# Six multiplications first, then the transfers of the next gates: reordering one stretch of a windowed-attention and expert layer

## The chip, the cores and the metric

The kernel runs on one core of one Trainium2 chip. The metric is the device time of one execution in microseconds. The kernel before was run three times: 4276.44, 4277.0 and 4289.2 us, median 4277.0. One more execution was taken with the profiler; all readings of a trace are of that one.

## The reference

The input is an image of 2 x 128 channels x 256 x 256 in f32. One layer is computed, everything in f32:

```python
x = x + attention(_ln_c(x))      # normalized over the 128 channels
t = _to_tokens(x)                # 131072 tokens of 128 channels
t = t + experts(_ln_t(t))
```

`attention` projects queries, keys and values by 1x1 convolutions. Queries stand in windows of 8 x 8 pixels, keys and values in windows of 12 x 12 around them, four heads of 32. Relative position terms are added, and a fixed mask lets a query see only the keys of its own row and column parity, so that each window falls into four independent ones of 16 queries and 36 keys. A softmax, the weighted values and an output projection follow. `experts` is a router over 8 experts: the softmax of `x @ router_w`, the two largest kept and scaled to sum 1, and

```python
out = sum over e of gate[e] * (x @ expert_w[e])
```

## The kernel before, in words

The image is cut into 64 strips of 8 rows; because of the mask a strip is worked in 4 *planes*, one for each parity of row and column, 512 pixels each. The loop at L980 runs over the 256 planes `n`. The bodies of one turn belong to different planes, so that the engines have something else to do while one of them waits: attention of plane `n` (`scores`, `attend`, `out_project`), the projections of plane `n+1` (`project`), the norms and the routing of a row pair of the strip before (`norms`, `route`), and the experts of row pairs that were routed one and two turns earlier (`ex`, `nxt`, `new`).

The order on every engine is the order of the code: the loop stands under a manual schedule for all five engines, and each engine takes its instructions in turn. All transfers of the loop are issued by SyncE (SP), also in turn. A transfer that waits for something holds back all behind it in SP's queue.

The experts are done without a gather. For a row pair (512 tokens), the gates are written to DRAM as rows of 512 values (`spread`, tile `gd`: 8 rows of gates, one for the mean, one for the rates of another row pair's norm). Each row is then read back to all 128 partitions, 256 KB a time:

- `fetch_rstd` (L629, tile `rb`): the rates, 1/deviation, with which GpSimd normalizes a row pair for the attention (`ln1`, L236).
- `fetch_means` (L658, tile `sb`, one buffer): the row that is added to the tokens to subtract their mean.
- `fetch(e)` (L652 and L653, tile `gb`, 8 buffers): gate `e`. Ahead of the transfer stands a tiny write to the tile, a memset on VectorE or a copy on ScalarE. It holds the transfer back until that engine has come to this place.

One turn later `means` (L663) makes `xs = tokens + sb`, `times(e)` (L669) makes `xe = xs * gb[e]` on VectorE for e = 0, 1, 2, 3, 4, 6 and on GpSimd for 5 and 7, and `product(e)` (L678) multiplies `xe` with the expert's matrix on TensorE, all eight accumulating in one PSUM tile. `end` (L684) adds the sum to the tokens.

The values of the attention also take a way through DRAM: `send_values` (L329) stores the value rows of plane `n+1` in `vrows`, and `take_values` (L341, two transfers of 240 KB, pieces of 512 bytes) gathers them by window in `vwin`, from which the next turn's `attend` reads them (L485).

TensorE's instruction stream is long: each plane has 128 small matmuls in `scores` (L454) and 128 in `attend` (L485). `nc.tensor.addr_align(BLOCK, ...)` at L995 pads the stream with NOPs so that the code of each turn stands at the same place within blocks of 256 instructions.

The turn's stretch that the change touches is this (L1039 to L1050): it follows `shift` (VectorE, L352 and L357) and the start of `attend` (the sums matmul L475 on TensorE), and is followed by the rest of `attend`, the load of new image rows (L117), gate 3, the store of finished rows (L716) and gates 4 and 6; gates 5 and 7 follow at the head of the next turn.

Of the kernel before, what the change touches and what calls it, by code (L numbers as in the profile page):

```python
# [52 lines left out]
def kernel(  # L53
# [270 lines left out]
    def send_values(n, sent):  # L324

        i, pl = divmod(n, 4)
        for part, vr in sent:
            for k, at, m in runs(i, part):
                nc.sync.dma_start(  # L329
                    vrows[pl][1 : PC + 1, at : at + m, :],  # L330
                    vr[:, k - part[0] : k - part[0] + m],
                )
# [92 lines left out]
    def scores(n, state):  # L425


        qs, kk, au = state["qs"], state["kk"], state["au"]
        turn = place(n // 4, 0) // 2
        att = ps_att.tile([P, 4, 512], F32, tag="att", name=f"att{n}")  # L430
        sc = att[:, :, 0:HQ]
        for w in range(2):
            for half in range(2):
                rows = slice(half * SLOT, (half + 1) * SLOT)
                for h in range(HEADS):
                    hp = slice(h * DH, (h + 1) * DH)
                    nc.tensor.matmul(  # L437
                        sc[rows, h].rearrange("p (t w z) -> p t w z", w=2, z=16)[:, :, w],
                        lhsT=keys[hp, turn, w],
                        rhs=au[hp, half * NP + w : (half + 1) * NP : 2].rearrange(  # L440
                            "p t a s -> p t (a s)"
                        ),
                        start=(w == 0),
                        stop=False,
                    )
        for t in range(HP):
            if t == HP // 2:
                yield
            for h in range(HEADS):
                hp = slice(h * DH, (h + 1) * DH)  # L450
                for half in range(2):
                    rows = slice(half * SLOT, half * SLOT + NK)
                    m0 = 2 * (half * HP + t)
                    nc.tensor.matmul(  # L454
                        sc[rows, h, 32 * t : 32 * t + 32],
                        lhsT=kk[hp, half * HP + t, 0:NK],
                        rhs=qs[hp, m0 : m0 + 2].rearrange("p m a s -> p (m a s)"),
                        start=False,
                        stop=(t == HP - 1),
                    )  # L460
        pT = work.tile([P, HEADS, HQ], F32, tag="pT", name=f"pT{n}", bufs=1)
        nc.scalar.activation(pT, att[:, :, 0:HQ], AF.Exp)  # L462
        state.update(att=att, pT=pT)
        yield
# [44 lines left out]
    def out_project(n, state):  # L509

        i, pl = divmod(n, 4)
        po = mm_tile(f"po{n}")
        nc.tensor.matmul(  # L513
            po, lhsT=wo, rhs=state["o"].rearrange("p f z -> p (f z)"), start=True, stop=True
        )
        yield
        xv = xt[i].rearrange("p (a y) (m s x) -> p y x m a s", y=2, x=2, s=4)[:, pl // 2, pl % 2]
        nc.vector.tensor_add(xv, po.rearrange("p (m a s) -> p m a s", a=PR, s=4), xv)
        yield
# [92 lines left out]
    def spread(f, c, g, nm):  # L612

        gT = small.tile([P, 2, 32], F32, tag="gT", name=f"gT{nm}")
        nc.vector.transpose(
            gT.rearrange("p k i -> p (k i)"), g.rearrange("p k b j -> p (k b j)")
        )
        gd = dram.tile([2 * E * NT, P], F32, tag="gd", name=f"gd{nm}")

        to = gd.rearrange("(k j t) (b i) -> k (t b) j i", k=2, j=E, i=32)  # L620
        for k in (1, 0):
            if k or f:
                nc.sync.dma_start(to[k], gT[:, k])
        return gd
# [262 lines left out]
    def row_at(n):  # L887

        i, pl = divmod(n + 2, 4)
        for j, k in ((i + 1, pl + 2), (i + 2, pl - 2)):
            if 0 < j < len(strips) and k in ln_rows(j) and (k > 1 or strips[j][1] == 0):
                return j, k
        return None
# [78 lines left out]
    gated, ex, nxt = None, NoExperts(), NoExperts()  # L974
    last = ctile([P, 1], "last")
    pool, dve = nc.gpsimd, nc.vector

    ET = mybir.EngineType
    with tc.manual_schedule(engines={ET.PE, ET.DVE, ET.Activation, ET.Pool, ET.SP}):
        for n in range(n_planes):  # L980
            i, pl = divmod(n, 4)
            score, attn, outp, ahead, norm, rout = none, none, none, none, none, none
            if n < n_planes:
                score = scores(n, states[n])
                attn = attend(n, states[n])
                outp = out_project(n, states[n])
            if n + 1 < n_planes:
                states[n + 1] = {}
                ahead = project(n + 1, states[n + 1])

            late = n == 6 or n > 6 and row_at(n) is None
            if n > 6 and row_at(n - 1) is not None:
                nc.tensor.addr_align(BLOCK, offset=BLOCK - FIRST_LIMIT)  # L995


            next(score, None)
            new, row = NoExperts(), None
            if gated and gated[0]:  # L1000
                rout = route(*gated[0], *gated[2])
            next(rout, None)
            nxt.fetch(5, nc.scalar)
            for _ in rout:
                pass
            next(score, None)
            next(ahead, None)
            nxt.fetch(7, nc.scalar)
            if gated:
                f, c, made = gated  # L1010
                gd = spread(f, c, made[0], f"_{n}")
                new = Experts(*f, gd) if f else new
            if n + 1 < n_planes:
                send_values(n + 1, states[n + 1]["sent"])
            if gated and c:
                row = (*c, fetch_rstd(gd, f"_{n}"))
            next(ahead, None)
            if n + 1 < n_planes:
                states[n + 1]["shift"]()
            filling = n < FILL  # L1020
            if not filling:
                next(ahead, None)
                next(ahead, None)
            for e in (4, 6, 7, 5):
                ex.product(e)
            if late:
                nc.tensor.addr_align(BLOCK, offset=SUMS_AT)


            f = (i - 1, pl) if 0 < i <= len(strips) else None  # L1030
            c = row_at(n)
            if f or c:
                room = None
                if filling:
                    room = ps_acc.tile([P, 512], F32, tag="acc", name=f"plt_{n}")
                norm = norms(f, c, f"_{n}", room)
            next(norm, None)
            next(attn, None)
            nxt.means()  # L1039
            new.fetch_means()  # L1040
            if n + 1 < n_planes:
                take_values(n + 1)
            for e in (0, 1, 2, 3):
                nxt.times(e, dve)
            new.fetch(0, dve)
            for e in (4, 6):
                nxt.times(e, dve)
            new.fetch(1, dve)
            ex.end()
            new.fetch(2, dve)  # L1050
            next(attn, None)
            next(attn, None)


            ex = nxt
            next(norm, None)
            if filling:
                next(ahead, None)
                next(ahead, None)
            load_x((n + 9) // 4, (n + 9) % 4, paced=True)  # L1060
            new.fetch(3, dve)
            while to_store:
                store(*to_store.pop())
            next(ahead, None)
            ex.product(0)
            made = next(norm, None)
            ex.product(1)
            ex.product(2)
            new.fetch(4, nc.scalar)
            nxt.behind(6)  # L1070
            nxt.times(5, pool)
            if row:
                ln1(*row, pool)
            if pl == 3 and i + 2 < len(strips):
                halo(i + 2)
            nxt.times(7, pool)
            if n + 2 < n_planes:
                borders(n + 2)
            next(outp, None)
            ex.product(3)  # L1080
            next(outp, None)
            new.fetch(6, dve)
            gated, nxt = (f, c, made) if made else None, new
            states.pop(n, None)

        finish_last(ex, nxt, gated)
# [59 lines left out]
```

## Time and profile before

| | |
|---|---|
| time, median of three runs | 4277.0 us |
| profiled execution: its time | 4283.76 us |
| profiled execution: its span | 4281.9 us |
| mean granted TensorE clock | 0.995 |
| TensorE busy | 4207.7 us, 98% |
| VectorE busy | 3787.3 us, 88% |
| ScalarE busy | 1315.1 us, 31% |
| GpSimd busy | 1072.3 us, 25% |
| moved by DMA | 1022.15 MB, 239 GB/s |
| a turn of the loop, median | 16.25 us |

The span runs from the first instruction to the last; the time of an execution holds about 2 us around it. A busy share of the whole span says which engine is used most, not where it waits: for that the waits, the chain of work that ended last and the timeline are read. In a line of waits stand the engine and the line that waited, what ended the wait, the total in us, how often, and the longest one. "issue" as the cause means that the engine waited for no semaphore that the profile shows.

### The profile page before, as it was taken

What the parts mean: (1) busy time and instruction counts of PE and PEld (TensorE: products, weight loads), DVE (VectorE), ACT (ScalarE), POOL (GpSimd) and SP (SyncE); (2) the same over time, 40 slices, a digit from 0 to 9 for tenths busy, and PEclk for the clock granted to TensorE, in tenths of its full rate; (3) what the DMA queues carried; (4) which work ended last, traced back from release to release, by engine and by line L of the source; (5) the groups of instructions that cost most, each with busy time, mean ns of one, the idle gap of its engine ahead of it and who ended that gap; (6) DMA issues with size and microseconds to landing.
All of it is one profiled execution on the core that took longest, in us unless ns stands there. A gap on an engine that the chain in (4) does not pass through costs nothing.

```text
span 4281.9 us, 224026 instructions
## 1 busy us (share of the span) xinstructions
PE 4207.7 (98%) x94273; PEld 2456.8 (57%) x94273; DVE 3787.3 (88%) x11768; ACT 1315.1 (31%) x3750; POOL 1072.3 (25%) x1109
## 2 busy tenths in 40 slices
PE   7999999999999999999999999999999999999998
PEld 5555555555555555555555555555555555555554
DVE  5888988989889898889888889898889998998998
ACT  3332323233333333333333333333333333233320
POOL 1222222222222222222222222222222222222220
PEclk9999999999999999999999999999999999999999
DMA  4877877878777877787878787877787777778776
GB/s 117 243 233 239 245 242 242 247 239 250 238 245 241 250 237 246 237 246 238 251 237 246 238 247 241 248 238 244 238 248 239 248 243 244 245 243 246 239 233 219
DMA packets 824576, 1022.15 MB, mean 239 GB/s; under 512 B 137634, under 2 KB 409634, under 8 KB 823594
## 3 DMA queue, kind: packets, MB, share of 16 engines
q1 hardware_dynamic: 822864, 1007.52, 76.1%
q8 instruction: 769, 12.60, 1.3%
q14 instruction: 213, 1.74, 0.1%
q10 hardware_dynamic: 730, 0.29, 0.0%
HBM read 863.78 MB, written 143.75 MB: 235 GB/s over the span
## 4 chain that ended last, share of the span: by engine, by line
PE 97%; issue 1%; DVE 1%; DMA 1%; SPq 0%; ACT 0%; DVEq 0%
PE acc L678 41%; PE att L454 8%; PE att L485 7%; PE pv L310 7%; PE plt L544 6%; PE pu L369 5%; PE po L513 5%; PE pk L383 5%; PE pq L408 5%; PE att L437 4%; PE att L475 3%; PE accl L766 0%; DMA gl<-gd_l 0%; DMA gb<-gd 0%; PE pltn L253 0%
## 5 line engine op out<-in xcount | busy, mean ns | idle before, releaser
L678 PE MATMUL acc<-xe,ew 128*128 128x512 f32 x4016 | 1874.6, 598 | 5.5 <-issue 5.0
L678 PEld LDWEIGHTS acc<-xe,ew 128*128 128x128 f32 x4016 | 740.6, 189 | 902.6 <-issue 852.2
L669 DVE TENSOR_TENSOR xe<-xs,gb 128x512 f32<-128x512 f32 x1508 | 932.5, 685 | 8.6
L673 POOL COPY last<-xe 128x1 f32<-128x1 f32 x250 | 45.9, 184 | 3021.0 <-DVE gb L652 3021.0
L669 POOL TENSOR_TENSOR xe<-xs,gb 128x512 f32<-128x512 f32 x500 | 635.8, 1272 | 1.5 <-PE att L485 1.2
L454 PE MATMUL att<-qs,kcol 32*60 32x32 f32 x32768 | 394.4, 222 | 24.2 <-issue 23.8
L454 PEld LDWEIGHTS att<-qs,kcol 32*60 32x60 f32 x32768 | 388.5, 126 | 28.9 <-issue 27.9
L236 POOL TENSOR_TENSOR xn<-xt,rb 128x512 f32<-128x512 f32 x249 | 374.3, 1503 | 101.9 <-DMA rb<-gd 100.4
L485 PEld LDWEIGHTS att<-pT,vwin 64*32 64x32 f32 x32768 | 351.5, 105 | 53.2 <-issue 15.6
L485 PE MATMUL att<-pT,vwin 64*32 64x32 f32 x32768 | 350.5, 201 | 12.1 <-issue 10.4
L462 ACT ACTIVATE pT<-att 128x1024 f32<-128x1024 f32 x256 | 262.0, 1024 | 264.3 <-PE att L454 264.1
L310 PE MATMUL pv<-wt,xn 128*128 128x128 f32 x2048 | 299.6, 290 | 0.0
L537 ACT ACTIVATE sq<-xt 128x512 f32<-128x512 f32 x501 | 290.2, 630 | 0.0
L357 DVE STREAM_TRANSPOSE au<-auT 128x512 f32<-128x512 f32 x256 | 269.6, 1053 | 8.8
L394 ACT COPY kcol<-pk 128x560 f32<-128x560 f32 (+2 forms) x344 | 183.0, 532 | 293.5 <-PE pk L383 290.7
L373 DVE STREAM_TRANSPOSE uT<-pu 128x512 f32<-128x512 f32 x256 | 183.3, 716 | 97.8 <-PE pu L369 93.8
L408 PE MATMUL pq<-xn,wt 128*128 128x512 f32 x512 | 263.0, 594 | 4.0 <-issue 4.0
L369 PE MATMUL pu<-xn,wrel 128*128 128x512 f32 x512 | 264.5, 598 | 0.0
L383 PE MATMUL pk<-xn,wt 128*128 128x512 f32 (+2 forms) x528 | 263.4, 582 | 0.0
L513 PE MATMUL po<-o,wt 128*128 128x512 f32 x512 | 262.1, 593 | 1.0 <-DVE gb L652 0.7
L310 PEld LDWEIGHTS pv<-wt,xn 128*128 128x128 f32 x2048 | 250.5, 193 | 10.6 <-DVE xn L236 0.2
L437 PEld LDWEIGHTS att<-au,keys 32*64 32x64 f32 x8192 | 115.8, 131 | 194.8 <-PE po L513 189.3
(2448 smaller groups left out, 4915.7 us busy)
## 6 DMA issues: line engine op xcount, KB each, us to landing
gb<-gd SPq DMA_DIRECT2D x2008, 256.0 KB, 5.7
vwin<-vrows SPq DMA_DIRECT2D x512, 240.0 KB, 4.9
xt<-in_x_dram SPq DMA_DIRECT2D x256, 256.0 KB, 6.5
out_dram<-xt SPq DMA_DIRECT2D x256, 256.0 KB, 6.1
sb<-gd SPq DMA_DIRECT2D x251, 256.0 KB, 4.5
rb<-gd SPq DMA_DIRECT2D x249, 256.0 KB, 3.4
vrows<-vr SPq DMA_DIRECT2D x168, 256.0 KB, 3.6
vrows<-vr SPq DMA_DIRECT2D x160, 128.0 KB, 3.5
```

The source lines that it names most:

```text
L236: eng.tensor_tensor(xn[i % 2][:, :, :, k, 1 : PC + 1], ln1_src(i, k).rearrange("p (y j x) -> p y x j", y=2, x=2), rb.rearrange("p (y j x) ...
L310: nc.tensor.matmul(pv[:, j * P : (j + 1) * P], lhsT=xp[:, k, 1 : PC + 1], rhs=wv, start=True, stop=True,)
L369: nc.tensor.matmul(pu, lhsT=wrel, rhs=inner, start=True, stop=True)
L383: nc.tensor.matmul(pk[:, : m * PC], lhsT=wk, rhs=xp[:, part[0] : part[0] + m, 1 : PC + 1], start=True, stop=True,)
L408: nc.tensor.matmul(pq, lhsT=wq, rhs=inner, start=True, stop=True)
L437: nc.tensor.matmul(sc[rows, h].rearrange("p (t w z) -> p t w z", w=2, z=16)[:, :, w], lhsT=keys[hp, turn, w], rhs=au[hp, half * NP + w : ( ...
L454: nc.tensor.matmul(sc[rows, h, 32 * t : 32 * t + 32], lhsT=kk[hp, half * HP + t, 0:NK], rhs=qs[hp, m0 : m0 + 2].rearrange("p m a s -> p (m ...
L485: nc.tensor.matmul(av[hp, half, 32 * t : 32 * t + 32], lhsT=vv[rows, t, hp], rhs=pT[rows, h, 32 * t : 32 * t + 32], start=True, stop=True,)
L513: nc.tensor.matmul(po, lhsT=wo, rhs=state["o"].rearrange("p f z -> p (f z)"), start=True, stop=True)
L537: nc.scalar.activation(sq, src, AF.Square)
L669: eng.tensor_tensor(self.xe[e], self.xs, self.gb.pop(e), ALU.mult)
L678: nc.tensor.matmul(self.acc, lhsT=ew[:, e, :], rhs=self.xe.pop(e), start=(e == 0), stop=not self.xe)
```

## The change

`take_values`, `fetch(0)`, `fetch(1)` and `fetch_means` move behind the six multiplications of VectorE. Before, the means and the two transfers of value rows stood ahead of the multiplications in the code, gate 0 after four of them and gate 1 after six. After, nothing is issued between the rates (`fetch_rstd`) and the end of the six; then gate 0, the value rows, gate 1, the means and gate 2 follow. What each of them moves, and the tiles and the number of instructions, stay as they are.

```diff
             nxt.means()
-            new.fetch_means()
+            for e in (0, 1, 2, 3, 4, 6):
+                nxt.times(e, dve)
+            new.fetch(0, dve)
             if n + 1 < n_planes:
                 take_values(n + 1)
-            for e in (0, 1, 2, 3):
-                nxt.times(e, dve)
-            new.fetch(0, dve)
-            for e in (4, 6):
-                nxt.times(e, dve)
             new.fetch(1, dve)
+            new.fetch_means()
             ex.end()
             new.fetch(2, dve)
```

## The prediction

> **What bounds the kernel now.** I read the page's shares first, then the chain that ended last.
>
> ```profile
> span 4281.9 us, 224026 instructions
> PE 4207.7 (98%) x94273; PEld 2456.8 (57%) x94273; DVE 3787.3 (88%) x11768; ACT 1315.1 (31%) x3750; POOL 1072.3 (25%) x1109
> ...
> q8 instruction: 769, 12.60, 1.3%
> ...
> PE 97%; issue 1%; DVE 1%; DMA 1%; SPq 0%; ACT 0%; DVEq 0%
> ```
>
> TensorE is 97% of the chain. In the chain in order of time a plane repeats every 16.24 us, and its matmuls stand end to end. With the matmul work unchanged, a gain can only come out of TensorE's idle time. TensorE's own waits show whose it is:
>
> ```profile
> PE att L454 <- issue: 23.8, 34, 3.8
> PE att L485 <- issue: 10.4, 17, 4.0
> ...
> PE acc L678 <- issue: 5.0, 8, 1.0
> ```
>
> "issue" means that no semaphore was waited for. One such gap, in the timeline of TensorE:
>
> ```profile
> 3157.43 0.36 PE L454 MATMUL att<-qs,kcol 32*60 32x32 f32 x17
> 3158.71 1.31 PE L454 MATMUL att<-qs,kcol 32*60 32x32 f32 x111 [0.92 <-issue]
> ```
>
> It falls inside a loop, always at the same matmul. The queue of kind "instruction" explains it: 12.60 MB in 769 packets is 16 KB each, three a plane, and TensorE's program is 768 rows a plane (the padding of `addr_align` included). So TensorE's code arrives in blocks of 256 rows. By the trace's packets a gap ends about 1.45 us after the block's packet has ended (here the packet ran 3156.40 to 3157.33).
>
> Let T be the start of the first sums matmul (L475) of a plane; all times behind T are medians over 242 steady planes. Blocks begin at T+1.61 (in L485), T+8.07 (in L454) and T+14.17 (in L678), and the packet of the next one starts after each of these points (from about 1 us before the third, where TensorE's sequencer runs ahead of slow matmuls). I name the packets by the moment they go:
>
> - A starts at T+4.0 (5% to 95%: 2.8 to 6.2), must end by 8.07 - 1.45 = T+6.6, and ends at T+5.3.
> - B starts at T+11.1 (10.2 to 12.0), must end by T+12.7, and ends at T+12.1.
> - C starts at T+15.0 (13.9 to 16.0), must end by T+16.4, and ends at T+16.2.
>
> Summed over 242 planes, the time by which they end too late is A 20.6, B 11.3, C 7.9 us, together 39.8. The planes exceed a floor of 16.246 us by 45.9 us in all, so these packets are nearly all there is to win: at best about -46 us (1.1%).
>
> What makes a packet late is the data in front of it. Busy time by stretches of one plane (T = 2030.08) has, in its last two columns, the DMA share and GB/s:
>
> ```profile
> 2028.70:2031.50 2.80, 2.80 (x129) 1.66 (x128) 2.80 (x8) 0.00 (x0) 0.00 (x0) 1.00 0.47 125
> 2031.50:2034.00 2.50, 2.50 (x79) 1.75 (x66) 2.40 (x6) 0.00 (x0) 2.15 (x3) 1.00 0.71 176
> 2034.00:2037.00 3.00, 3.00 (x8) 1.14 (x6) 2.31 (x12) 0.47 (x3) 2.31 (x3) 1.00 0.98 246
> 2037.00:2041.00 4.00, 4.00 (x170) 3.14 (x170) 3.58 (x17) 1.79 (x5) 0.00 (x0) 1.00 1.05 385
> 2041.00:2043.30 2.30, 2.30 (x7) 1.10 (x6) 2.13 (x6) 1.40 (x4) 0.00 (x0) 1.00 0.78 257
> ```
>
> A goes in the light part, B in the full one (1.05), C as it empties. The queue that issues, in the timeline:
>
> ```profile
> 3148.09 0.33 SPq L629 DMA_DIRECT2D rb<-gd  x1
> 3148.52 1.33 SPq L658 DMA_DIRECT2D sb<-gd  x1
> 3149.96 0.90 SPq L341 DMA_DIRECT2D vwin<-vrows  x2
> 3150.96 1.42 SPq L653 DMA_DIRECT2D gb<-gd  x3
> 3152.42 1.51 SPq L117 DMA_DIRECT2D xt<-in_x_dram  x1
> ```
>
> **The change, part by part.** No instruction is added or removed; DVE, SP and nothing else change order (in the built program SP's order becomes rates, gate 0, value rows twice, gate 1, means, gate 2).
>
> DVE: two memsets of 59 ns move behind multiplications 4 and 6. The six multiplications end 0.06 us sooner. Value nothing; TensorE needs those products at T+12.
>
> SP: issue starts now stand at T-1.4 rates, -0.95 means, +0.8 and +1.3 values, +1.8 gate 0, +2.3 gate 1, +2.75 gate 2, +3.2 x, +4.5 gate 3. The sixth product ends at T+1.4, and an issue takes about 0.45 us, so I get T-1.4 rates, nothing until +1.45, then gate 0 +1.45, values +1.9 and +2.35, gate 1 +2.8, means +3.25, gate 2 +3.7, x +4.15, gate 3 +4.6. From gate 3 on the queue is where it was; its waits for ACT and DVE set the rest. SP's wait for the stored value rows (L341, 173.4 us in 183 waits) falls into the hole and costs nothing.
>
> Data in time: means land at T+3.7 and are read one plane later, at T+13.2; landing some 6 us later they would still have 3 us. Value rows land at T+5.2 and 6.7, are read at T+16.8, and move by 1 us. Gate 1 has 5 us. I price these at 0; each us beyond that cover would cost DVE a us a plane, 250 us in all, so the cover has to be gone entirely before it counts. Rates come behind the code and gates of the plane before; POOL waited for them in 32 of 249 cases already, and its product 7 is used 8 us later: 0.
>
> Packet A: its request leaves near T+1.0 (idle engines at startup served one 1.1 us after, the earliest A starts at T+2.0). In front of it now stand means (land T+3.7) and values. A's start follows the landing of the means by 0.90 us per us (correlation 0.62). Means and values now come behind it, so A starts near T+2.5 and is never late. Bounds: 0 and -20.6. I take **-20**.
>
> Packets B and C: what is not moved in the hole is moved later. The means are 256 KB, 128 packets of 2 KB at 84 ns on 16 engines, 0.7 us of every engine; the values, 0.8 us each, begin 1 us later; about 0.4 us of idle engine share between T+3 and T+7 gives some back. So the full part is 0.5 to 1.0 us deeper. The trace has a natural trial: the fifth of the planes in which the values' issue ended last (T+1.6 to 2.6; after the change T+2.35 to 2.8). There A starts at T+3.4 instead of 4.0, B at 11.56 instead of 11.14, C at 15.35 instead of 14.99, and the plane exceeds the floor by 0.26 us, the next by 0.31, against 0.19 on average. Bounds for B: 0 (the queue is full either way), and a shift of 0.7 us, which by the trace's own distribution of ends costs 70 - 11 = +58. By the trial's late planes B is 0.141 us too late on average, 34 us over 242: **+23**. C: 0 by the trial's own C (0.033 us, as elsewhere), +32 by shifting all ends by 0.4 us (40 - 8): between them, **+16**.
>
> Sum: -20 + 23 + 16 = **+19 us** on the profiled execution's 4283.8, so 4303; the three runs' median is 4277.0, 6.8 lower, so 4296.
>
> Two rules bear on this, and none of the numbers above use them. "Runtime: NRT & Kernel Launch" of the Trainium skill, section "Instruction fetch mechanics", says that code streams in 16 KiB blocks and that crossing into one is mostly hidden; the block size agrees with 12.60 MB in 769, the hiding does not (39.8 us), and by it the sum would be 0. "DMA: Bandwidth & Descriptors", in its paragraph "Arbitration", lets each engine take turns between queues packet by packet, so that code would wait for one packet of data and not for the backlog; then B and C would not move, and the sum would be -20. The natural trial (B 0.42 us later behind a deeper queue) speaks for the backlog.
>
> **The rivals.** A measurement here tells about 0.3% (13 us) from no change.
>
> - Backlog moves on to B and C, the forecast: 4285 to 4325. Chance 0.45.
> - The other side, faster: B and C wait no longer behind a deeper queue than a full one, and only A moves. For it: B goes at full load in both kernels; planes with the values issued at T+1.1 to 1.4 have the smallest excess (0.03 to 0.11 us). Against: the late fifth. It decides if B's start moves by less than about 0.15 us. -20: 4257. Chance 0.27.
> - A wash: A's 20 us and about as much in B and C, or the means' place filled by idle engines: 4264 to 4290 with the middle 4277. Chance 0.18.
> - The deeper end: B 0.7 and C 0.5 us later: -20 + 58 + 46 = +84, 4361, damped since a longer plane gives the transfers time: about 4345. Chance 0.10.
> - The hole is not one: the rates, issued at T-1.4, land at T+2.1, and a late store of value rows can stand in it. Then A gains half; contained in the cases above.
>
> **How the numbers follow.** The likeliest case gives 4296. The range takes the faster rival's middle at its low end, half of that rival lying below, and the deeper end at its top: 4257 to 4340. Faster by over 0.3%: 0.26. Within: 0.21. Slower: 0.53.
>
> **What would show it.** Right: in the waits of TensorE the gaps at L454 go from 23.8 us to some 5 and those at L678 rise from 5.0 to over 20, at L485 above 10.4; in the stretch T-0.1 to T+1.4 the DMA share falls, from T+7 to T+12 it stays near 1 and lasts longer. The faster rival: L454 empty, the others as they were. Wrong altogether: DVE or POOL waits for sb, gb or rb that were not there, TensorE waiting for xe, or L454's gaps unchanged.

## The result, and the profile after

The changed kernel takes 4306.91 us (median of four runs, 4305.39 to 4308.77); the kernel before took 4276.72 beside it. The ratio is 1.0067, 95% interval 1.0052 to 1.0083: slower by 0.7%, or 30 us (22 to 35 by the interval). The profiled executions are 4283.76 and 4305.39 us, only 21.6 apart: that of before lies 7 us above its kernel's median, and that of the changed kernel is the fastest of its four.

The page and TensorE's own waits of the changed kernel (who waited, for what: total us, times, longest):

```profile
span 4303.6 us, 223943 instructions
PE 4210.9 (98%) x94273; PEld 2453.3 (57%) x94273; DVE 3795.5 (88%) x11768; ACT 1316.2 (31%) x3750; POOL 1076.7 (25%) x1109
...
PE 97%; issue 2%; DVE 1%; DMA 0%; SPq 0%; ACT 0%; DVEq 0%
```

```profile
PE acc L678 <- issue: 21.5, 35, 1.9
PE att L485 <- issue: 18.1, 44, 3.4
PE att L454 <- issue: 12.7, 17, 5.2
```

Nothing was added to TensorE's work, and in the steady planes it waits for no gate, mean or value row. Its gaps moved: L454, where block A comes too late, from 23.8 to 12.7 us; L678, block B, from 5.0 to 21.5; L485, block C, from 10.4 to 18.1. These three lines together went from 39.2 to 52.3 us. Where a gap is too short to be listed as a wait it still lengthens the plane, so the better account is the packets themselves: the time by which they end too late, over some 240 steady planes (C against the start of the next plane), went from A 20.6, B 11.3, C 7.9 to A 12.2, B 29.7, C 19.3, from 39.8 to 61.2. That is 21.4 us, and the span of these two executions grew by 21.7. (The trace of a second run of the changed kernel, reported below, has about 6, 30 and 18 by the same count: single cells of such a count differ by some 6 us between executions.)

Busy time by stretches of one plane of the changed kernel (T = 1993.99; the same places in the plane as the stretches of before; the last two columns are DMA share and GB/s):

```profile
1992.61:1995.41 2.80, 2.80 (x126) 1.65 (x126) 2.80 (x8) 0.00 (x0) 0.00 (x0) 1.00 0.29 100
1995.41:1997.91 2.50, 2.50 (x79) 1.76 (x67) 2.40 (x6) 0.00 (x0) 2.27 (x3) 1.00 0.59 168
1997.91:2000.91 3.00, 3.00 (x8) 1.14 (x6) 2.31 (x12) 0.47 (x3) 1.88 (x2) 1.00 0.83 214
2000.91:2004.91 4.00, 4.00 (x171) 3.26 (x171) 3.58 (x17) 1.91 (x5) 0.00 (x0) 1.00 0.95 348
2004.91:2007.21 2.30, 2.30 (x7) 1.01 (x6) 2.08 (x5) 1.23 (x5) 0.00 (x0) 1.00 1.03 375
```

The hole is there (0.47 became 0.29; in the stretch T-0.1 to T+1.4, which the prediction named, 0.74 became 0.15), and it is paid at the other end: the last stretch, in which the DMA engines were emptying at 0.78, is now full at 1.03. SP's timeline in that plane shows the new order, and that the rates came late:

```profile
1993.99 0.33 SPq L629 DMA_DIRECT2D rb<-gd  x1
1995.44 0.32 SPq L653 DMA_DIRECT2D gb<-gd  x1
1995.86 0.90 SPq L341 DMA_DIRECT2D vwin<-vrows  x2
1996.85 0.40 SPq L653 DMA_DIRECT2D gb<-gd  x1
1997.30 0.42 SPq L658 DMA_DIRECT2D sb<-gd  x1
1997.78 0.42 SPq L653 DMA_DIRECT2D gb<-gd  x1
```

### The profile page after: what moved, and what is told of

Its sections match the earlier page's. It is cut to its first block, busy times and chain, and to the rows that moved or that the text cites. A ratio compares the mean times of both kernels' runs of the same rounds, so it can differ in the third digit from the quotient of the medians.

```text
span 4303.6 us, 223943 instructions
## 1 busy us (share of the span) xinstructions
PE 4210.9 (98%) x94273; PEld 2453.3 (57%) x94273; DVE 3795.5 (88%) x11768; ACT 1316.2 (31%) x3750; POOL 1076.7 (25%) x1109
## 4 chain that ended last, share of the span: by engine, by line
PE 97%; issue 2%; DVE 1%; DMA 0%; SPq 0%; ACT 0%; DVEq 0%
PE acc L678 41%; PE att L454 8%; PE att L485 7%; PE pv L310 6%; PE plt L544 6%; PE pk L383 5%; PE po L513 5%; PE pq L408 5%; PE pu L369 5%; PE att L437 4%; PE att L475 3%; PE accl L766 0%; DMA gl<-gd_l 0%; DVE xe L669 0%; PE pltn L253 0%
## 5 line engine op out<-in xcount | busy, mean ns | idle before, releaser
L678 PE MATMUL acc<-xe,ew 128*128 128x512 f32 x4016 | 1882.0, 598 | 22.8 <-issue 21.5
L678 PEld LDWEIGHTS acc<-xe,ew 128*128 128x128 f32 x4016 | 740.0, 189 | 929.0 <-issue 879.2
L236 POOL TENSOR_TENSOR xn<-xt,rb 128x512 f32<-128x512 f32 x249 | 374.3, 1503 | 187.3 <-DMA rb<-gd 156.3
L454 PE MATMUL att<-qs,kcol 32*60 32x32 f32 x32768 | 389.2, 222 | 12.7 <-issue 12.7
L454 PEld LDWEIGHTS att<-qs,kcol 32*60 32x60 f32 x32768 | 385.5, 126 | 15.1 <-issue 14.4
L485 PEld LDWEIGHTS att<-pT,vwin 64*32 64x32 f32 x32768 | 353.0, 105 | 64.1 <-issue 27.4
L485 PE MATMUL att<-pT,vwin 64*32 64x32 f32 x32768 | 354.6, 200 | 20.6 <-issue 18.1
L310 PEld LDWEIGHTS pv<-wt,xn 128*128 128x128 f32 x2048 | 248.6, 191 | 10.6 <-DVE xn L236 0.2
L495 DVE STREAM_TRANSPOSE sT<-att 128x512 f32<-128x512 f32 x256 | 183.5, 717 | 67.6 <-PE att L485 66.0
```

Of the source, the lines that this page charges most:

```text
L236: eng.tensor_tensor(xn[i % 2][:, :, :, k, 1 : PC + 1], ln1_src(i, k).rearrange("p (y j x) -> p y x j", y=2, x=2), rb.rearrange("p (y j x) ...
L310: nc.tensor.matmul(pv[:, j * P : (j + 1) * P], lhsT=xp[:, k, 1 : PC + 1], rhs=wv, start=True, stop=True,)
L454: nc.tensor.matmul(sc[rows, h, 32 * t : 32 * t + 32], lhsT=kk[hp, half * HP + t, 0:NK], rhs=qs[hp, m0 : m0 + 2].rearrange("p m a s -> p (m ...
L485: nc.tensor.matmul(av[hp, half, 32 * t : 32 * t + 32], lhsT=vv[rows, t, hp], rhs=pT[rows, h, 32 * t : 32 * t + 32], start=True, stop=True,)
L678: nc.tensor.matmul(self.acc, lhsT=ew[:, e, :], rhs=self.xe.pop(e), start=(e == 0), stop=not self.xe)
```

## The experiments

Every experiment was compared with the kernel before on its own chip. Each row of this table sums, over the steady planes of the one profiled execution, the time by which blocks A, B and C ended behind the same limits as above. The ratios are from all timed executions. The profiled one is 7 us slower than its kernel's median in the row of before and faster than it in six others (in five of them the fastest of all), so for the total the ratios count, and these sums for where it is lost:

| kernel | ratio to before, 95% | A | B | C |
|---|---|---|---|---|
| before | 1 | 20.6 | 11.3 | 7.9 |
| changed | 1.0067 (1.0052 to 1.0083) | 12.2 | 29.7 | 19.3 |
| changed, means early | 1.0097 (1.0083 to 1.0111) | 28.3 | 32.2 | 18.2 |
| changed, value rows early | 1.0034 (1.0022 to 1.0047) | 4.3 | 17.6 | 10.8 |
| hole filled, means late | 1.0031 (1.0019 to 1.0042) | 4.7 | 22.3 | 11.9 |
| changed, image rows in the hole | 1.0044 (1.0031 to 1.0058) | 8.5 | 16.7 | 16.0 |
| changed, no means | 1.0039 (1.0026 to 1.0051) | 5.8 | 17.9 | 12.9 |
| before, no means | 0.9952 (0.9939 to 0.9964) | 1.3 | 5.3 | 3.3 |
| before, image rows early | 0.9997 (0.9985 to 1.0008) | 21.6 | 2.2 | 3.3 |
| before, means at once | 1.0002 (0.9992 to 1.0013) | 14.3 | 12.4 | 5.9 |

**Which of the moves costs.** Two kernels undo one part each.

```diff
 # means early
             nxt.means()
+            new.fetch_means()
             for e in (0, 1, 2, 3, 4, 6):
 ...
             new.fetch(1, dve)
-            new.fetch_means()
```

> The changed order, but with the means issued where they stood before, right behind the rates; the value rows, gates 0 and 1 stay behind the six multiplications. Backlog theory (what is moved out of the hole makes blocks B and C of TensorE's code late): the means are 0.7 us of every DMA engine, about a third of what was moved; 4285 to 4297, TensorE's gaps at L678 down from 21.5 us to about 12, those at L454 up. Rival (the value rows alone decide, the means only changed places with gate 0): 4302 to 4310. Second rival (the hole is good and the means' late place is not the cause): above 4307.

It gave 1.0097, no faster than the changed kernel (1.0067, and 1.0072 when it was run again; the intervals touch or overlap), and it lies where the second rival had it. TensorE's waits:

```profile
PE att L454 <- issue: 23.5, 43, 5.2
PE att L485 <- issue: 16.4, 36, 4.0
PE acc L678 <- issue: 5.6, 17, 0.8
```

The gaps at L678 went, as expected, but those at L454 are back at 23.5, so the sum is not: the means stand in front of A again, and the value rows still run late. B's own packets are as late as before the edit (B starts at T+11.58); with A late in front, TensorE arrives at B's block later and waits less there. With A's lateness in the same plane taken off, B is 14.9 us too late instead of 32.2, while in the two traces of the changed kernel this takes off 2 to 4 us. My figure for this kernel was wrong, and with it the idea that every transfer taken out of the late part makes B earlier: with the means early and the value rows late, B did not move. Why not is not shown.

```diff
 # value rows early
             nxt.means()
+            if n + 1 < n_planes:
+                take_values(n + 1)
             for e in (0, 1, 2, 3, 4, 6):
                 nxt.times(e, dve)
             new.fetch(0, dve)
-            if n + 1 < n_planes:
-                take_values(n + 1)
             new.fetch(1, dve)
```

> The changed order, but with the value rows issued where they stood before, ahead of the six multiplications; means, gates 0 and 1 behind them. Backlog theory: two thirds of what was moved is back; 4278 to 4290, gaps at L678 about 8 us, at L454 about 20 us. Rival (the means decide): 4300 to 4310.

Half of the loss is gone, and the rival with the means fell.

```profile
PE att L485 <- issue: 10.4, 22, 3.4
PE acc L678 <- issue: 9.5, 22, 0.8
PE att L454 <- issue: 7.8, 8, 3.0
```

With the means late and the value rows early, A is in time (7.8 us at L454, where I had expected about 20; most of it before the steady planes), B and C are a little later than before. So of what stood in front of A it was the means that made it late, and late value rows cost B and C more than late means. The five timed runs (4277.91 to 4287.82) say 1.0034; the profiled one is the fastest of them, so the table's row flatters it.

**Closing the hole.** Value rows ahead, gates 0 and 1 marked sooner than in the kernel before, means last. The stretch then reads:

```python
             nxt.means()
             if n + 1 < n_planes:
                 take_values(n + 1)
             nxt.times(0, dve)
             new.fetch(0, dve)
             nxt.times(1, dve)
             new.fetch(1, dve)
             for e in (2, 3, 4, 6):
                 nxt.times(e, dve)
             new.fetch_means()
```

> The hole closed instead of opened: value rows ahead of the multiplications as before, gate 0 right behind multiplication 0 (before: behind 3), gate 1 right behind multiplication 1 (before: behind 6), the means behind all six. Same transfers. Backlog theory (the time that the DMA engines lose in the hole is what makes code blocks B and C late): nothing waits for a multiplication that it does not need, the full part ends earlier than in the kernel before, ratio 0.993 to 0.999, gaps at L678 under 5 us. Rival (the late means cost by themselves, as value rows early and means late gave 1.0034): 1.002 to 1.005.

The expectation fell and the rival's range was met: 1.0031, no better than the row above. Gates 0 and 1 are issued at T+1.6 and T+2.1, behind the value rows in SP's queue, against T+1.75 and T+2.24 in the kernel before, so setting their marks earlier gains only 0.15 us. What is left of the edit are the late means, and they go with 0.3%; that this is because they have to pass in the full part is argued, not tried.

**The code itself.** Is TensorE held up by late code, or does the late code only stand beside late data? This kernel moves no transfer, only the padding:

```diff
-BLOCK, FIRST_LIMIT, SUMS_AT = 256, 99, 40
+BLOCK, FIRST_LIMIT, SUMS_AT = 256, 107, 40
```

> The changed kernel with no transfer moved: only the padding of TensorE's code is shifted by 8 rows (FIRST_LIMIT 107 in place of 99), so that the block that begins at T+14.17 in the products begins two products later, near T+15.0; the other two boundaries move by about 0.04 us. If TensorE's loss is code that arrives late: B has 0.86 us more and is never late, so the gaps at L678 go (about -20 us). C is asked for 0.86 us later: if its start is set by the data in front of it, it moves little and the time is 4285 to 4297; if its start follows the request, its ends move by 0.86 us and the time is 4380 or more, with the gaps at L485. Rival (the loss is late data, not late code): 4304 to 4310, gaps where they were.

```profile
PE att L485 <- issue: 32.7, 56, 3.4
PE att L437 <- issue: 16.4, 1, 16.4
PE att L454 <- issue: 7.6, 7, 3.2
```

The 21.5 us at L678 are gone without a transfer being moved: TensorE waits there for code and nothing else. They reappear in part at L485 (18.1 to 32.7), although C starts at T+15.50 against 15.39: with the boundary 0.86 us later it moved by 0.1 (the request itself is not in the trace), which fits a start set by the data in front of it. TensorE, no longer held at L678, comes to C's block sooner, so that C now ends some 40 us too late in all instead of 19. The steady planes exceed the floor of 16.246 us by 57 us, against 68 and 63 in the two traces of the changed kernel. The ratio, 1.0102 (1.0087 to 1.0118), has in it one gap of 16.4 us, a padding of 248 NOPs where the first alignment no longer fitted; without it, it would be near 1.0064, hardly better than the changed kernel. So the forecast of the place came in, that of the time did not. I tried to take the gap away by moving the other constant along:

```diff
-BLOCK, FIRST_LIMIT, SUMS_AT = 256, 99, 40
+BLOCK, FIRST_LIMIT, SUMS_AT = 256, 107, 32
```

> The changed kernel with the code boundary in the products two products later, as after_lim107, but with SUMS_AT lowered by the same 8, which takes away one padding of 248 NOPs (16.4 us in one place) that after_lim107 had. After_lim107 without it would be at about 1.0064. Code theory: B's gaps gone and C's up, together about -10 us against the changed kernel, ratio 1.003 to 1.006. Rival (late data, not late code): as the changed kernel, 1.006 to 1.009.

It did not: the padding only moved to the sums, and the ratio is 1.008 (1.0062 to 1.0098).

```profile
PE att L485 <- issue: 31.7, 66, 2.9
PE att L475 <- issue: 20.9, 5, 15.9
PE att L454 <- issue: 11.6, 12, 4.9
```

For the place of the waits both kernels are clear (again none at L678); the steady planes exceed the floor by 51 us here, and the 15.9 come on top. The changed kernel, run beside it once more:

> The changed kernel once more, beside the others on one chip, since the earlier runs were on another: ratio to before 1.005 to 1.009 by every theory.

It gave 1.0072 (1.0053 to 1.0092), with 19.4 us at L678, 16.7 at L485, 10.5 at L454.

**The amount.** The means' transfer is left out, once of the changed kernel and once of the kernel before:

```diff
-            self.sb = gates.tile([P, NT * P], F32, tag="sb", ...)
-            nc.sync.dma_start(self.sb, to_all(self.gd, E))
+            self.sb = sb_one
```

(`sb_one` is a tile of zeros that is written once at the start; `...` marks what is left out of a line or between lines.)

> The changed kernel without the transfer of the means: a tile of zeros stands in for them, so the tokens' mean term is left out of the experts; every other transfer and instruction stays. It takes 64 MB of 1022 away, 0.7 us of every DMA engine in each turn. Backlog theory: B and C come about 0.4 us earlier, 4270 to 4285, gaps at L678 about 6 us, at L485 about 10 us. Rival (the order and the hole matter, not the amount): 4300 to 4310.

> The kernel before without the transfer of the means (zeros stand in for them, so the tokens' mean term is left out of the experts), order otherwise as before. Backlog theory: 256 KB less in each turn, and what is taken away stood in front of code block A: A starts near T+3.0 and its gaps at L454 (23.8 us) fall to under 8, B and C come earlier too; ratio 0.990 to 0.996. Rival (the amount does not matter, only what is held back by the hole): 0.999 to 1.001.

Both are faster than with means: the changed kernel by 0.3%, the kernel before by 0.5% (0.9952, as expected). The changed kernel's 1.0039 lies between its two forecasts, with gaps of 14.3 us at L678 and 13.7 at L485 where 6 and 10 were expected. In the kernel before without means all three blocks come nearly in time:

```profile
PE att L485 <- issue: 7.1, 7, 3.4
PE att L454 <- issue: 6.0, 5, 3.2
PE acc L677 <- issue: 3.8, 9, 0.8
```

(L677 is the products' line, one line up in this kernel.) B starts at T+10.61 instead of 11.14, A at 3.52 instead of 3.99. So the amount of data counts, with the order untouched. But the order counts as well: without means in either kernel the change costs 0.9% (0.9952 to 1.0039), no less than with them. The loss is therefore not made by the late means alone; late value rows and gates 0 and 1 are enough. The opposite trial failed to be one:

```diff
             nc.sync.dma_start(self.sb, to_all(self.gd, E))
+            nc.sync.dma_start(self.sb, to_all(self.gd, E))
```

> The kernel before, with the transfer of the means issued twice in a row to the same tile: 256 KB more in each turn, 64 MB in all, order and hole as before. Backlog theory: 0.7 us more on every DMA engine, as taking the same 256 KB out of the changed kernel gave about -0.3%: ratio 1.003 to 1.008, with the gaps at L678 and L485 up. Rival (the place of the hole matters and not the amount): 0.999 to 1.002.

The ratio is 1.1602 (1.1578 to 1.1627), of another cause. The waits of SP, VectorE and TensorE:

```profile
SPq L659 <- DMA sb<-gd: 821.4, 251, 4.7
DVE xe L670 <- DMA gb<-gd: 361.4, 543, 2.3
PE att L485 <- issue: 356.3, 242, 3.5
```

The second transfer to the same tile waits for the first to land, 3.3 us in each turn, and SP's whole queue stands behind it. VectorE then waits for gates, which it did not in the kernel before, and TensorE waits at L485 in 242 turns, by the place and the kind of the wait for block C: its largest wait in this kernel, too, is for code. The run says nothing on 0.7 us of load, only what a wait in SP's queue costs.

**Other uses of the idle part.** In the kernel before, the image rows' load moves ahead of the rates:

```diff
+            load_x((n + 9) // 4, (n + 9) % 4, paced=False)
             if gated and c:
                 row = (*c, fetch_rstd(gd, f"_{n}"))
 ...
-            load_x((n + 9) // 4, (n + 9) % 4, paced=True)
```

> The kernel before with one transfer moved: the load of new image rows (256 KB) goes ahead of the rates, some 5 us earlier, into the part where the DMA engines empty, and without its copy on ScalarE that held it back. Nothing else moves. Backlog theory: 0.7 us of every engine leaves the full part, B and C about 0.4 us earlier, A as before or a little later: ratio 0.994 to 0.999, gaps at L678 and L485 down. Rival (A is what counts, and a transfer ahead of it makes it late): 1.001 to 1.005, gaps at L454 up.

```profile
PE att L454 <- issue: 30.1, 37, 6.8
PE att L485 <- issue: 8.2, 7, 2.9
PE acc L678 <- issue: 0.8, 2, 0.6
```

Something of both theories is seen in one kernel: B starts at T+10.58 and its gaps at L678 are gone, C's fell, and A's rose from 23.8 to 30.1 (by the packets A hardly changed, 21.6 against 20.6). The time is the same, 0.9997, outside both ranges. In the changed kernel the same load is put into the hole, right behind the rates:

> The changed kernel with the load of new image rows moved into the hole, right behind the rates, without the copy on ScalarE that held it back: the hole is used, all else stays behind the multiplications. Backlog theory: 0.7 us of every engine comes back, B and C 0.4 us earlier, A later: ratio 1.002 to 1.005 (the changed kernel 1.0072 on this chip). Rival (the late gates, value rows and means cost by themselves): 1.006 to 1.009. Second rival (as means_back: what stands in the hole makes A late and saves nothing): 1.008 to 1.011.

1.0044: 0.2 to 0.3% come back, as forecast (the intervals overlap a little), and A did not suffer. But B and C did not come 0.4 us earlier: they start at T+11.50 and 15.34 against 11.56 and 15.39, and only the latest of them are gone (95% of B start by T+12.1 instead of 12.4). The last one issues the means of the kernel before at once behind the rates, with a second buffer, so that they need not wait for VectorE's addition:

```diff
             if gated and c:
                 row = (*c, fetch_rstd(gd, f"_{n}"))
+            new.fetch_means()
 ...
             nxt.means()
-            new.fetch_means()
```

> The kernel before with two buffers for the means and their transfer issued at once behind the rates, without waiting for VectorE's addition; about 0.5 us earlier. Backlog theory: A's start follows the landing of the means (0.9 us per us before), so A comes 0.3 to 0.5 us earlier, as do B and C a little: ratio 0.995 to 0.999. Rival (this wait was not in the way): 0.999 to 1.001.

No difference (1.0002), as the rival said: the means land at T+3.40 instead of 3.70, A starts 0.15 us sooner, and what it gains (20.6 to 14.3) is within what two executions of one kernel differ by (A of the changed kernel: 12.2 and 6.0).

No kernel that computes the whole layer was found to beat the kernel before.

## Why the prediction was right, and where its terms were off

The cause was the forecast one, and so was the sign: 4296 with a range of 4257 to 4340, measured 4306.91. The +19 of the sum lies a little under the measured interval, 22 to 35 us; by the two profiled executions, on which the terms are read, it is 21.6. That the sum came so near is in part luck, as the terms show:

- **A, -20 forecast, -8 measured** (20.6 to 12.2; -15 in the second trace). I had A start near T+2.5 in a free hole. A quarter of the planes does (T+2.3 to 2.5), as many start behind T+5.1. The hole is not free. The rates come later: they are issued at T-0.25, not at T-1.4, and land at T+3.0. SP waits at their line for the gates' rows to land in DRAM,

```profile
SPq L629 <- DMA gd<-gT: 487.7, 247, 4.4
...
SPq L653 <- DMA vwin<-vrows: 251.2, 327, 2.4
SPq L653 <- DMA sb<-gd: 105.2, 223, 2.0
```

  against 279.3 us before, since that landing is at the end of the same backlog. What I took for a fixed edge of the hole depends on what the hole does. Planes with the rates issued by T-0.5 have A at 2.46, those behind T+0.24 at 4.8. This goes together within one trace; no run moved the rates alone.
- **SP "from gate 3 on the queue is where it was": wrong.** Gate 3 goes at T+5.5 (forecast 4.6), the store at 6.2, gates 4 and 6 at 7.4 and 8.5, each 1.0 to 1.3 us later than before. The lines above show why: SP waits for the landing of value rows and means. In most of the planes whose landings the trace tells (about half of all), gate 4 goes 0.06 us behind the landing of the first value rows, and gates 6 and 5 as closely behind those of the second ones and of gate 1, each the eighth transfer back; in none does one go sooner. So a late transfer delays not only what lies behind it in the engines but also the issues.
- **B, +23 forecast, +18 measured; C, +16 forecast, +11.** B starts at 11.56 and C at 15.39, where the late fifth of the planes of before had 11.56 and 15.35. The natural trial in the old trace told these two medians to 0.04 us, but not A's (3.4 there, 4.2 measured). C's price was only the middle of two bounds. That A gained 12 us less and B and C cost 10 us less than forecast cancelled, by luck.
- **0 for late data** held: among TensorE's waits only the first planes' and the last rows' name data. POOL waited for rates more often, 127 times instead of 32 (156.3 us instead of 100.4), and no engine's waits name POOL.

On the two rules of the Trainium skill: "Instruction fetch mechanics" ("Runtime: NRT & Kernel Launch") calls the crossing mostly hidden; here late blocks cost 40 to 60 us of some 4300, and that moves with the data. "Arbitration" ("DMA: Bandwidth & Descriptors"), a turn between queues packet by packet, would leave B where it is when the data queue is deeper or shallower. B stood at 10.6 with less data or the image rows sooner, at 11.1 before, at 11.6 after (but also at 11.6 with the means back in the hole). How the engines choose between the code's queue and the data's was not tried by itself and stays open.

The rival of the faster side, that only A moves, fell with B's 0.4 us. It was half right in one respect: a transfer in front of A can cost what A loses, as the means put back into the hole showed (28.3 us); the early image rows (21.6) and the image rows in the hole (8.5) did not show it.

## What to carry to other kernels

Where an engine is busy to 98%, look at its gaps that wait for no semaphore: if they come at the same instruction each time, its code may be arriving behind data, and then the order and the amount of transfers cost time although no data is late. Here, opening a pause for one fetch of code did not pay, since what was held back made the next two late; sending less data helped every fetch at once. The planes that happen to look like the changed kernel are a trial that the old trace already holds: here it told B and C, but not A.

## What was not expected of the hardware

The start of a code block seems to follow the data in front of it more than its own place in the code: with the boundary 0.86 us later, block C came 0.1 us later. In the changed kernel three transfers of each turn waited in SP's queue for the landing of the eighth one before them, and went 0.06 us behind it in most planes. And a second write to the same tile, 3.3 us of waiting in SP's queue per turn, made the whole kernel 16% slower, since all transfers of the loop stand in that one queue.
